# Refitting the transfer times and priorities of a planner that orders a four-layer graph network on one core

## The chip, the core and the metric

The kernel runs on one of the eight cores of a Trainium2 chip. The time is device microseconds of one launch. Five engines work side by side, each through its own instructions in order: TensorE (PE) for matrix products and transposes, VectorE (DVE), ScalarE (ACT), GpSimd (POOL), and SyncE (SP), which here only issues transfers. POOL issues some transfers too.

## The reference, cut to what matters

There are 16 graphs of 1024 nodes with 256 features, and one adjacency matrix for all. Four layers follow each other, and each adds its result to its input.

```python
for W, a in (L0, L1, L2):                        # 4, 1 and 1 heads
    h = max(layernorm(x), 0)
    q = h @ W
    e = leaky_relu(q @ a_src [:, None] + q @ a_dst [None, :])
    x = x + act(softmax(where(adj > 0, e, -big)) @ q)     # elu, relu, elu
h = max(layernorm(x), 0)                         # layer 3: a transformer block
q, k, v = split(h @ w_qkv)                       # 8 heads of 32
p = softmax(where(adj > 0, q @ k.T / sqrt(32), -1e9))
y = layernorm(h + p @ v) * g1 + c1
x = x + layernorm(y + relu(y @ w1 + b1) @ w2 + b2) * g2 + c2
```

## The kernel before

All of it is in fp32. The graphs ("batches", `b` from 0 to 15) are handled one by one, in tiles of 128 nodes (`NT` = 8) and halves of 512 nodes (`hf`).

- `gat` (layers 0 to 2) normalizes and transposes the features (L502, L531, L766), projects them (L772) and exponentiates the scores of single nodes (L783). The scores of one side become a row: PE transposes them (L838), SP writes them to DRAM (`turn_rows`, L845) and reads them back onto all 128 partitions (`spread`, L854). DVE makes the masked weights `pt` from the row (`weights`, L870). In layers 1 and 2 PE multiplies them with the features as a full array (L897). In layer 0 it runs column-tiled: four products of 32 columns stand side by side (L984 for values, L994 for the softmax's sums).
- `attention` (layer 3) keeps a copy of its input in DRAM first (`end`, L1637). `project` makes queries and keys (L1134), which are split into a high part (`hi`, L1143 on ACT) and a rest (`lo`, L1146 on DVE). Both go to a DRAM buffer `hl` (L1152), and four transfers read them back as stacks `ks` or `qs` of four 32-row pieces (L1158), so that one single-pass product of 128 rows gives a head's scores. `values` makes the values (L1172). A step is one tile of keys, one half of queries and four heads: scores (L1355), exponentials (L1379, ACT), mask (L1388, DVE), and, two steps later, values (L1220, column-tiled). For the softmax's sums, the masked weights of two or four steps are added up before one column-tiled product with ones: the first two steps on DVE (L1247), the others by an accumulating transfer from POOL's queue (L1256). In the last batch each step has its own product with ones.
- `feed` normalizes (L437 to L502), transposes, applies the two feed-forward products (L1452, with L1473 on ACT and L1490 on DVE), transposes back, reads the layer's input from DRAM (`xr`, L1505, with L1511 on DVE), normalizes again, and writes the result (L1577). `xr` has two buffers, so a read waits for an earlier write of the result.

Nothing runs in the order of this text. Every call of `pe`, `act`, `dve`, `pool` or `dma` is recorded as a piece of work with a planned duration, its operands and a stream. `Record.schedule` then simulates the five queues and gives each engine a fixed order, in which the instructions are emitted. It takes the piece that can start first; among those that can start at the same time, the one with the lowest key. What it reads:

- `KNOTS` gives each kind of stream its key along its length, added to the batch number. So 1.0 means "one batch later". "gat0" to "gat2" are layers 0 to 2, "beside" is layer 0 of batch 1 (which runs in borrowed buffers at the start), "values" is the opening of layer 3 (normalization, projections, stacks), "steps" its steps, "feed" the feed-forward, "last" that of the last batch. `LEAD` lowers the key of ACT's and DVE's pieces.
- `PASS` is the time from the planned end of a piece to the start of one on another engine that waits for it.
- `SWITCH` is what a change between column-tiled and other matmuls adds to PE's planned time. `BIAS` times it is added to the key of a piece that would need the change.
- A transfer has `moved`, for which it holds a queue common to all, and `lands`, until its data is there. `SLACK` is added to that. SP's issue takes 0.57 us in the plan, POOL's 1.135. If the queue is over `BEHIND` (2.0) behind, SP's issue takes `HELD` (1.35):

```python
queue = max(at + (us if e == "pool" else 0.2), queue) + x.moved
x.pass_on = queue + x.lands + SLACK - (at + us)
```

Of the kernel before, what the change touches and what calls it, by code (L numbers as in the profile page):

```python
# [113 lines left out]


WEIGHT = {"pe": 1.0, "dve": 0.3}
PASS = {"pe": 0.122, "act": 0.556, "dve": 0.232, "pool": 0.13, "dma": 0.0}


class Work:  # L120


    def __init__(self, engine, us, emit, key, modes, moved, lands):
        self.engine, self.us, self.emit, self.key, self.modes = engine, us, emit, key, modes
        self.pass_on = PASS[engine]
        self.moved = moved
# [9 lines left out]
def priority(x):  # L136
# [3 lines left out]
    key = base + knots[k] + (knots[k + 1] - knots[k]) * (at - k)  # L140
    return round(key - (LEAD.get(x.engine, 0.0) if lead else 0.0), 6)


class Record:
# [44 lines left out]
    def schedule(self):  # L189
        for n, x in enumerate(self.work):  # L190
# [4 lines left out]
            for y in x.before:  # L195
                y.after.append(x)
        free = dict.fromkeys(PASS, 0.0)
        queue = 0.0
        future = {e: [] for e in PASS}
        now = {e: [] for e in PASS}  # L200
        mode = "full"
# [15 lines left out]
        def turn(x):  # L217

            return BIAS * SWITCH.get((mode, x.modes[0]), 0.0) if x.engine == "pe" else 0.0

# [20 lines left out]
        while True:  # L241
            choices = [(c, e) for c, e in ((choose(e), e) for e in PASS) if c]
            if not choices:
# [16 lines left out]
            if x.moved:  # L260
                if e == "dma" and queue - at > BEHIND:
                    us = max(us, HELD)
                queue = max(at + (us if e == "pool" else 0.2), queue) + x.moved
                x.pass_on = queue + x.lands + SLACK - (at + us)
            order.append(x)
# [14 lines left out]


BEHIND, HELD = 2.0, 1.35
SLACK = 0.722
KNOTS = {
    "gat0": (-10.926, -10.742, -7.218, -4.626, -2.628, -2.099, -0.444, -3.636, -2.816),
    "gat1": (0.191, 0.25, 0.454, 0.45, 0.566, 0.582, 0.633, 1.016, 0.672),
    "gat2": (1.126, -0.076, -0.221, -0.062, 0.894, -0.428, 0.959, 1.018, 1.17),
    "beside": (1.093, 3.374, 4.836, 2.176, 5.971),
    "values": (1.444, -1.53, -3.682, -3.253, 0.902, 0.891, 2.874, 0.851, 0.421),
    "steps": (0.98, 1.188, 1.323, 1.512, 1.578, 1.712, 2.006, 2.02, 1.489),  # L290
    "feed": (2.026, 2.163, 1.768, 1.658, 2.343, 1.828, 2.009, 2.223, 3.042),
    "last": (3.521, -0.495, 0.103, 1.329, 1.339, 5.969, 5.585, 3.41, 5.439),
}
BIAS = 2.241
LEAD = {"act": 8.212, "dve": 0.635}

SWITCH = {
    ("full", "col4"): 0.137,
# [7 lines left out]
def act_us(n, pointers=0, sbuf=0):  # L306
    return (n / 1.2 + 41 + 50 * sbuf + 101 * pointers) / 1000


def tt_us(n):  # L310
    return (n / 0.96 + 67) / 1000
# [10 lines left out]
def mm_us(n):  # L322
    return 2 * max(2 * n / 2.4 + 3.0, 109) / 1000
# [5 lines left out]
def direct(ctx, tc, flag, x, adj, gat_w, gat_a, w_qkv, ln1_g, ln1_b, ln2_g, ln2_b, w1, b1, w2, b2, out):  # L329


    nc = tc.nc
# [87 lines left out]
    def pe(us, emit, w, r, modes=("full", "full")):  # L420
        rec.add("pe", us, emit, w, r, modes)

    def act(us, emit, w, r):
        rec.add("act", us, emit, w, r)

    def dve(us, emit, w, r):
        rec.add("dve", us, emit, w, r)
# [4 lines left out]
    def dma(moved, lands, emit, w, r, key=None, us=0.57, engine="dma"):  # L432
        rec.add(engine, us, emit, w, r, key=key, moved=moved, lands=lands)
# [293 lines left out]
    def gat(xt, b_mv, b_rstd, l, my):  # L727
# [120 lines left out]
        def spread(hf, h, rd):  # L848

            row = my.row.new()  # L850
            dma(
                1.2,
                2.07,
                lambda: nc.sync.dma_start(  # L854
                    row.t,
                    rd.t[h * TH : (h + 1) * TH, :]
                    .rearrange("t n -> (t n)")
                    .partition_broadcast(P),
                ),
                [row],  # L860
                [rd],
            )
            return row
# [21 lines left out]
        for hf in range(2):  # L885
            s = slice(hf * TH, (hf + 1) * TH)
            if H == 1:
                row = spread(hf, 0, rds[hf])
                pts = [weights(hf, 0, jt, row) for jt in range(NT)]
                for k in range(TH):  # L890
# [56 lines left out]
                    if l == 1:  # L947
                        last, op = ex, ALU.add
                    else:
                        dve(tt_us(C), lambda: nc.vector.tensor_add(xs, xs, ex), [xt(it)], [b_ex(0)])  # L950
                        last, op = eo, ALU.subtract
# [132 lines left out]
    def attention(b, xt, b_mv, b_rstd):  # L1084
# [42 lines left out]
        def project(g, hf, keys, stack, at):  # L1127

            sc, hi, lo = r_sc.new(), r_hi.new(), r_lo.new()
            c0 = keys * C + g * P  # L1130

            def product():
                for ct in range(CT):
                    nc.tensor.matmul(  # L1134
                        sc.t,
                        wqkv_sb[:, ct, c0 : c0 + P],
                        hT.t[:, ct, hf * HALF : (hf + 1) * HALF],
                        start=ct == 0,
                        stop=ct == CT - 1,
                    )  # L1140

            pe(CT * mm_us(HALF), product, [sc], [b_qkv] + [hT((ct, hf)) for ct in range(CT)])
            act(act_us(HALF), lambda: nc.scalar.copy(hi.t.bitcast(F32R), sc.t), [hi], [sc])  # L1143
            dve(
                tt_us(HALF),
                lambda: nc.vector.tensor_sub(lo.t, sc.t, hi.t),  # L1146
                [lo],
                [sc, hi],
            )
            hl = r_hl.new()  # L1150
            for k, part in enumerate((hi, lo)):
                dma(0.65, 1.5, lambda: nc.sync.dma_start(hl.t[:, k, :], part.t), [hl(k)], [part])  # L1152
            for a in range(4):
                k = ((0, 0, 1, 1), (0, 1, 0, 1))[keys][a]
                dma(
                    1.0,
                    1.83,
                    lambda: nc.sync.dma_start(  # L1158
                        stack.t[a * D3 : (a + 1) * D3, :, at : at + HALF],
                        hl.t[:, k, :].rearrange("(r d) n -> d r n", r=HG),  # L1160
                    ),
                    [stack((r, hf if keys else 0, a)) for r in range(HG)],
                    [hl(k)],
                )
# [28 lines left out]
        def queries(g, hf):  # L1193
            qs[g, hf] = r_qs.new()
            project(g, hf, 0, qs[g, hf], 0)
# [19 lines left out]
        steps = [(g, hf, jt) for g in range(CT) for hf in range(2) for jt in range(NT)]  # L1215
# [12 lines left out]
        def run_of(g, hf):  # L1228

            return 1 if b == NB - 1 else 4 if hf == 1 else 2  # L1230
# [4 lines left out]
        for n in range(len(steps) + LAG):  # L1235
            m = n - LAG
            if m >= 0:
                g, hf, jt = steps[m]
                if jt == 0:
                    accs[g, hf] = [r_bank.new(), r_bank.new()]  # L1240
                run = run_of(g, hf)
                if jt % run == 1:
                    sums[g, hf] = [r_sums.new() for _ in range(2)]
                    for ss, p0, p1 in zip(sums[g, hf], pas[m - 1], pas[m]):
                        dve(
                            tt_us(2 * HALF),
                            lambda: nc.vector.tensor_add(ss.t, p0.t, p1.t),  # L1247
                            [ss],
                            [p0, p1],
                        )  # L1250
                elif jt % run:
                    for ss, pt in zip(sums[g, hf], pas[m]):
                        dma(
                            2.8,
                            0.85,
                            lambda: nc.gpsimd.dma_start(ss.t, pt.t, accum_op=ALU.add),  # L1256
                            [ss],
                            [pt],
                            us=1.135,
                            engine="pool",  # L1260
                        )
                pe(
                    0.8585,
                    lambda: quad(
                        accs[g, hf][0],
                        lambda r: pas[m][r // 2].t[:, r % 2, :],
                        lambda r: va.t[:, jt, (g * HG + r) * D3 : (g * HG + r + 1) * D3],
                        jt == 0,
                        jt == NT - 1,
                    ),  # L1270
                    [accs[g, hf][0]],
                    pas[m] + [va(jt)],
                    ("col4", "col4"),
                )
                if jt % run == run - 1:
                    ss = pas[m] if run == 1 else sums[g, hf]
                    pe(
                        0.8585,
                        lambda: quad(
                            accs[g, hf][1],  # L1280
                            lambda r: ss[r // 2].t[:, r % 2, :],
                            lambda r: ones,
                            jt == run - 1,
                            jt == NT - 1,
                        ),
                        [accs[g, hf][1]],
                        ss,
                        ("col4", "col4"),
                    )
# [111 lines left out]
    def feed(b, x3, hn):  # L1401
# [95 lines left out]
        def back(hf):  # L1497
            yT = yTs[hf]
            for it in (hf * TH, hf * TH + 2):
                g, z, mvz, rstdz = r_bank.new(), r_fz.new(), r_mvz.new(), r_rstdz.new()  # L1500
                xr = r_xr.new()
                dma(
                    1.0,
                    1.83,
                    lambda: nc.sync.dma_start(xr.t, x3.t[:, it : it + 2, :]),  # L1505
                    [xr(0), xr(1)],
                    [x3(hf)],
# [763 lines left out]
```

## Time and profile before

| what | value |
|---|---|
| median of 3 runs | 4077.22 us (4068.27 to 4077.92) |
| the profiled execution | 4072.03 us, its span 4070.3 us |
| granted TensorE clock | 0.995 |
| transfers | 456.54 MB, mean 112 GB/s |
| first / last matmul | starts at 11.3 us / ends at 4059.8 us |

The span runs from the first to the last instruction of the profiled execution. "Busy" is the time in which at least one instruction of an engine runs; a transfer's issue isn't counted. Lines named L... are lines of the kernel before; the change adds and removes no line, so they are the same after it. In a list of waits, "A <- B" says that A's engine sat idle until B was done. In a timeline, the columns are start, duration, engine, line, operation and operands, and brackets hold the idle time before it and what ended it.

### The profile page before, as it was taken

What the parts mean: (1) busy time and instruction counts of PE and PEld (TensorE: products, weight loads), DVE (VectorE), ACT (ScalarE), POOL (GpSimd) and SP (SyncE); (2) the same over time, 40 slices, a digit from 0 to 9 for tenths busy, and PEclk for the clock granted to TensorE, in tenths of its full rate; (3) what the DMA queues carried; (4) which work ended last, traced back from release to release, by engine and by line L of the source; (5) the groups of instructions that cost most, each with busy time, mean ns of one, the idle gap of its engine ahead of it and who ended that gap; (6) DMA issues with size and microseconds to landing.
All of it is one profiled execution on the core that took longest, in us unless ns stands there. A gap on an engine that the chain in (4) does not pass through costs nothing.

```text
span 4070.3 us, 66071 instructions
## 1 busy us (share of the span) xinstructions
PE 4012.3 (99%) x23874; PEld 2352.0 (58%) x23874; DVE 3501.7 (86%) x5994; ACT 2666.6 (66%) x6673; POOL 621.0 (15%) x631
## 2 busy tenths in 40 slices
PE   7999999999999999999999999999999999999998
PEld 4566466564655646566564665646556465665643
DVE  7778898989989899898988989899898998989866
ACT  5467575775757767576675766757577675766765
POOL 1101111111111112111111111111111121111200
PEclk9999999999999999999999999999999999999999
DMA  3034454444545345463444544445543454624451
GB/s 128 27 103 115 126 126 109 113 104 115 124 125 123 83 117 126 115 150 76 126 110 123 127 110 113 104 115 122 127 121 82 117 128 115 150 69 121 112 137 51
DMA packets 227520, 456.54 MB, mean 112 GB/s; under 512 B 24688, under 2 KB 59760, under 8 KB 227184
## 3 DMA queue, kind: packets, MB, share of 16 engines
q1 hardware_dynamic: 192624, 326.39, 28.3%
q0 software_dynamic: 34560, 125.84, 16.2%
q8 instruction: 190, 3.11, 0.3%
q14 instruction: 146, 1.20, 0.1%
HBM read 225.25 MB, written 101.06 MB: 80 GB/s over the span
## 4 chain that ended last, share of the span: by engine, by line
PE 94%; DMA 3%; ACT 1%; DVE 1%; issue 0%; SPq 0%; DVEq 0%; ACTq 0%; POOLq 0%
PE bank L897 21%; PE bank L1220 16%; PE sc L1355 12%; PE bank L984 11%; PE bank L772 9%; PE bank L531 6%; PE sc L1134 5%; PE bank L1452 5%; PE bank L994 5%; PE sc L1172 3%; DMA sums<-pa 2%; PE sc L531 1%; DVE pt L870 1%; ACT waste L448 0%; ACT pa L1379 0%
## 5 line engine op out<-in xcount | busy, mean ns | idle before, releaser
L1388 DVE TENSOR_TENSOR pa<-pa,mask 128x1024 f32<-128x1024 f32 x1024 | 1222.7, 1219 | 166.1 <-ACT pa L1379 162.6
L1379 ACT ACTIVATE pa<-sc 128x512 f32<-128x512 f32 x2048 | 1101.6, 611 | 370.1 <-DVE sums L1247 174.4
L870 DVE SCALAR_TENSOR_TENSOR pt<-row,e,mask 128x512 f32<-128x512 f32 x1472 | 1011.9, 744 | 46.6 <-DMA row<-rd 27.7
L897 PE MATMUL bank<-qb,pt 128*128 128x257 f32 x4096 | 941.0, 380 | 0.0
L897 PEld LDWEIGHTS bank<-qb,pt 128*128 128x128 f32 x4096 | 770.6, 190 | 143.6 <-issue 20.1
L1355 PE MATMUL sc<-qs,ks 128*128 128x512 f32 x2048 | 727.9, 457 | 2.6 <-DMA hl<-hi 1.1
L1220 PE MATMUL bank<-pa,va 128*32 128x512 f32 x4096 | 515.0, 597 | 0.0
L1355 PEld LDWEIGHTS sc<-qs,ks 128*128 128x128 f32 x2048 | 361.3, 189 | 237.9 <-ACT pa L1379 82.5
L984 PE MATMUL bank<-pt,qb 128*32 128x512 f32 x3840 | 461.7, 596 | 6.5 <-DVE pt L870 6.5
L1247 DVE TENSOR_TENSOR sums<-pa,pa 128x1024 f32<-128x1024 f32 x360 | 434.1, 1220 | 16.7 <-PE bank L1220 14.2
L772 PE MATMUL bank<-w_aug,hT 128*128 128x259 f32 (+1 forms) x1504 | 373.3, 389 | 0.0
L1256 POOL DMA_DIRECT2D sums<-pa x240 | 211.5, 883 | 954.1 <-DVE pa L1388 426.6
L772 PEld LDWEIGHTS bank<-w_aug,hT 128*128 128x128 f32 x1504 | 280.3, 190 | 99.6 <-ACT qb L794 35.4
L925 ACT ACTIVATE ex<-bank,rec 128x256 f32<-128x256 f32 x256 | 121.4, 475 | 288.9 <-DVE rec L917 288.7
L984 PEld LDWEIGHTS bank<-pt,qb 128*32 128x32 f32 x3840 | 116.5, 110 | 294.8 <-issue 219.5
L1220 PEld LDWEIGHTS bank<-pa,va 128*32 128x32 f32 x4096 | 115.0, 109 | 250.6 <-issue 225.7
L994 PE MATMUL bank<-pt,e 128*32 128x512 f32 x1920 | 252.0, 593 | 0.1
L1134 PE MATMUL sc<-hTa,wqkv_sb 128*128 128x512 f32 x512 | 240.0, 596 | 0.0
L468 POOL TENSOR_TENSOR rstd<-rstd,neg_half 128x4 f32<-128x4 f32 x96 | 169.2, 1762 | 362.1 <-DVE rstd L460 362.0
L1143 ACT CAST hi<-sc 128x512 fp32r<-128x512 f32 x128 | 75.1, 587 | 211.8 <-PE sc L1134 122.0
L502 ACT ACTIVATE hn<-xh,mv,rstd 128x256 f32<-128x256 f32 x376 | 202.8, 613 | 7.5 <-DVE mv L492 4.1
L1220 PE MATMUL bank<-sums,ones 128*32 128x512 f32 x1440 | 200.5, 600 | 3.9 <-DMA sums<-pa 3.7
(152 smaller groups left out, 4501.0 us busy)
## 6 DMA issues: line engine op xcount, KB each, us to landing
sums<-pa POOLq DMA_DIRECT2D x240, 512.0 KB, 6.0
ks<-hl SPq DMA_DIRECT2D x256, 256.0 KB
qs<-hl SPq DMA_DIRECT2D x256, 256.0 KB
row<-rd SPq DMA_DIRECT2D x184, 256.0 KB
hl<-hi SPq DMA_DIRECT2D x128, 256.0 KB
hl<-lo SPq DMA_DIRECT2D x128, 256.0 KB
xh<-in_x_dram SPq DMA_DIRECT2D x32, 512.0 KB
x<-xh SPq DMA_DIRECT2D x32, 512.0 KB
```

The source lines that it names most:

```text
L531: nc.tensor.transpose(dst(k), src(k), ident[:shape, :shape])
L772: nc.tensor.matmul(g.t[:, : C + 3 * H], hT.t[:, ct, k * P : (k + 1) * P], w_aug[l][:, ct, :], start=ct == 0, stop=ct == CT - 1,)
L870: lambda: nc.vector.scalar_tensor_tensor(pt.t, row.t, e3[:, 2, jt // TH, h, jt % TH : jt % TH + 1], mask[:, jt, hf * HALF : (hf + 1) * HAL ...
L897: nc.tensor.matmul(g.t[:, : D + 1], pts[jt].t[:, k * P : (k + 1) * P], qb[:, jt, 0, :], start=jt == 0, stop=jt == NT - 1,)
L984: nc.tensor.matmul(g.t[u * D + d : u * D + d + D3, :], qb[:, j, h + u, d : d + D3], pts[u][j - jt].t, start=j == 0, stop=j == NT - 1,)
L994: nc.tensor.matmul(gd.t[c : c + D3, :], one(jt + k, h + u).to_broadcast([P, D3]), pts[u][k].t, start=jt == 0, stop=jt == NT - 2,)
L1134: nc.tensor.matmul(sc.t, wqkv_sb[:, ct, c0 : c0 + P], hT.t[:, ct, hf * HALF : (hf + 1) * HALF], start=ct == 0, stop=ct == CT - 1,)
L1220: nc.tensor.matmul(ac.t[r * D3 : (r + 1) * D3, :], columns(r), of_head(r), start=first, stop=last,)
L1247: lambda: nc.vector.tensor_add(ss.t, p0.t, p1.t),
L1355: nc.tensor.matmul(scs[r - r0].t, ks.t[:, r, jt * P : (jt + 1) * P].bitcast(F32R), q.t[:, r, :].bitcast(F32R), start=True, stop=True,)
L1379: lambda: nc.scalar.activation(pt.t[:, v, :], sc.t, AF.Exp, scale=1.0 / math.sqrt(D3)),
L1388: lambda: nc.vector.tensor_mul(pt.t, pt.t, mask[:, jt : jt + 1, i0 : i0 + HALF].to_broadcast([P, 2, HALF]),),
```

## The change

Only numbers that the planner reads are changed. Which instructions are emitted, and what each does, stays the same. Five kinds of transfer get other `moved` and `lands`: the row of scores, the write of a high or low part, the four reads of a stack, the accumulating transfer, and the read of a layer's input. All eight curves of keys change, and so do `PASS`, `SLACK`, `BIAS` and `LEAD`.

```diff
-PASS = {"pe": 0.122, "act": 0.556, "dve": 0.232, "pool": 0.13, "dma": 0.0}
+PASS = {"pe": 0.067, "act": 0.488, "dve": 0.242, "pool": 0.13, "dma": 0.0}
...
-SLACK = 0.722
+SLACK = 0.692
 KNOTS = {
-    "gat0": (-10.926, -10.742, -7.218, -4.626, -2.628, -2.099, -0.444, -3.636, -2.816),
-    "gat1": (0.191, 0.25, 0.454, 0.45, 0.566, 0.582, 0.633, 1.016, 0.672),
-    "gat2": (1.126, -0.076, -0.221, -0.062, 0.894, -0.428, 0.959, 1.018, 1.17),
-    "beside": (1.093, 3.374, 4.836, 2.176, 5.971),
-    "values": (1.444, -1.53, -3.682, -3.253, 0.902, 0.891, 2.874, 0.851, 0.421),
-    "steps": (0.98, 1.188, 1.323, 1.512, 1.578, 1.712, 2.006, 2.02, 1.489),
-    "feed": (2.026, 2.163, 1.768, 1.658, 2.343, 1.828, 2.009, 2.223, 3.042),
-    "last": (3.521, -0.495, 0.103, 1.329, 1.339, 5.969, 5.585, 3.41, 5.439),
+    "gat0": (-7.312, -4.53, -3.41, -4.841, -1.822, -0.301, 0.129, -1.248, -5.175),
+    "gat1": (-0.059, 0.15, 0.563, 0.572, 0.637, 0.706, 0.828, 0.909, 0.804),
+    "gat2": (0.909, 0.795, 0.647, 0.447, 0.883, 0.816, 0.664, 0.955, 1.033),
+    "beside": (-0.048, 0.945, 2.708, 2.827, 3.928),
+    "values": (0.436, -0.157, -3.896, -2.01, 0.718, 1.463, 1.194, -0.148, -1.52),
+    "steps": (0.888, 1.134, 1.481, 1.462, 1.63, 1.792, 2.109, 1.797, 1.607),
+    "feed": (2.034, 1.861, 1.224, 2.222, 2.01, 2.099, 2.853, 2.305, 2.94),
+    "last": (2.431, 3.84, 3.952, 4.83, 2.296, 3.947, 5.098, 5.097, 8.086),
 }
-BIAS = 2.241
-LEAD = {"act": 8.212, "dve": 0.635}
+BIAS = 1.297
+LEAD = {"act": 9.115, "dve": 1.117}
...
             dma(                        # spread: row<-rd
-                1.2,
-                2.07,
+                1.45,
+                1.75,
...
-                dma(0.65, 1.5, lambda: nc.sync.dma_start(hl.t[:, k, :], part.t), [hl(k)], [part])
+                dma(0.82, 1.67, lambda: nc.sync.dma_start(hl.t[:, k, :], part.t), [hl(k)], [part])
...
                 dma(                    # project: ks<-hl, qs<-hl
-                    1.0,
-                    1.83,
+                    1.15,
+                    2.18,
...
                         dma(            # sums<-pa
-                            2.8,
-                            0.85,
+                            2.4,
+                            2.0,
...
                 dma(                    # back: xr<-x
-                    1.0,
-                    1.83,
+                    1.3,
+                    1.6,
```

## The prediction

> **What bounds the kernel now.** I read the page's first two parts first, for the engine that is full, then the chain that ended last, then who TensorE (PE) waited for, then the timeline where those waits lie. From the page:
>
> ```profile
> span 4070.3 us, 66071 instructions
> PE 4012.3 (99%) x23874; PEld 2352.0 (58%) x23874; DVE 3501.7 (86%) x5994; ACT 2666.6 (66%) x6673; POOL 621.0 (15%) x631
> PE   7999999999999999999999999999999999999998
> PE 94%; DMA 3%; ACT 1%; DVE 1%; issue 0%; SPq 0%; DVEq 0%; ACTq 0%; POOLq 0%
> ```
>
> PE is busy from the second slice to the last but one, and 94% of the chain is PE. Since the ends of matmuls are modelled, 99% alone doesn't say that it runs at its peak. So I added up its work from the distances between starts of equal matmuls: 4096 of L897 at 0.2165 us are 887; 1492 column-tiled groups (8 matmuls of L1220, L984 or L994) at 0.860 are 1283; 2048 of L1355 at 0.231 are 473; 1536 of L772 at 0.218 to 0.222 are 337; 1024 of L1134 and L1452 at 0.429 are 439; 512 of L1172 at 0.216 are 111; 2720 transposes (L531, L838) at 0.109 are 296. Sum 3826 us, and no instruction is added or removed, so this part can't change. The other 244 us can: 58 in which PE is idle (4070.3 - 4012.3), and 186 inside "busy".
>
> Who PE waited for (us in total, times, longest):
>
> ```profile
> PE bank L531 <- DVE pa L628: 11.3, 1, 11.3
> PE bank L984 <- DVE pt L870: 6.5, 1, 6.5
> PE bank L531 <- DVE yT L1490: 6.0, 2, 3.0
> PE bank L531 <- ACT xh L502: 4.9, 1, 4.9
> ...
> PE bank L1220 <- DMA sums<-pa: 3.7, 7, 1.5
> PE bank L1452 <- ACT fz L1473: 2.6, 3, 1.4
> PE sc L1172 <- DVE lo L1146: 2.6, 2, 2.4
> PE sc L1355 <- DMA hl<-hi: 1.1, 1, 1.1
> ```
>
> Nearly all of it is at the two ends: 22.9 us before 50 us, 16.6 after 3850, and 10.5 after the last matmul. All waits on a transfer together are 5.4 us (3.7, 1.1, and 0.6 on qs). The middle, 100 to 3850 us, has no hole worth naming.
>
> The 186 us inside "busy" is mostly changes between column-tiled and other matmuls. The timeline of PE late in the last attention, where each step is two tiled groups and four scores:
>
> ```profile
> 3995.35 1.07 PE L1220 MATMUL bank<-pa,va 128*32 128x512 f32 x8
> 3996.24 1.04 PE L1220 MATMUL bank<-pa,ones 128*32 128x512 f32 x8
> 3997.21 1.19 PE L1355 MATMUL sc<-qs,ks 128*128 128x512 f32 x4
> 3998.33 1.06 PE L1220 MATMUL bank<-pa,va 128*32 128x512 f32 x8
> ```
>
> A period is 2.98 us (3998.33 - 3995.35); two groups and four scores alone are 2 x 0.860 + 4 x 0.231 = 2.64. Going into and out of the tiling thus costs 0.34 us a pair. Counted along the trace's matmuls there are 413 such pairs: 140 us, 3.4% of the span.
>
> **What the Trainium skill says.** "TensorEngine Tiling (Array Packing)", Key Properties, states that a change of tiling mode drains the array. The rows above agree, and set the price that I use: 0.34 us a pair. "Perfetto Trace Analysis", Tensor Engine Instruction, says that ACT and DVE take their instructions strictly in order, so what stands behind a waiting one waits too. The timeline of all engines shows just that in the hole at 3900 us:
>
> ```profile
> 3906.30 0.69 DVE L1511 TENSOR_TENSOR xr<-xr,row_c 128x512 f32<-128x512 f32 x1 [4.79 <-DMA xr<-x]
> 3906.91 0.16 DVE L492 SCALAR_TENSOR_TENSOR mv<-mv,rstd 128x4 f32<-128x4 f32 x1
> 3907.11 2.08 ACT L502 ACTIVATE xh<-xh,mv,rstd 128x256 f32<-128x256 f32 x4 [3.66 <-DVE mv L492]
> 3907.76 2.80 PE L531 MATMUL bank<-ident,xh 128*128 128x128 f32 x8 [4.93 <-ACT xh L502]
> ```
>
> VectorE (DVE) waits 4.79 us for a row of x; L492, whose input POOL wrote by 3902.6, stands behind it, then ACT, then PE. An order that puts L1511 there only fits a plan in which the row lands earlier; on the chip it shared the transfer engines with four stack transfers issued at 3901.89.
>
> **The change part by part.** The instructions and all emitted operands stay; only numbers that the planner reads differ. The order on every engine and queue (PE, ACT, DVE, POOL, and SP's transfers) comes out anew, and each instruction costs what its row shows, so the work sums to 0. What moves is holes and tiling pairs.
>
> *Transfer lengths and landings.* A lone transfer is planned to land 0.2 + moved + lands + SLACK after its issue. From the trace's landings: the accumulating transfer into sums lands 6.0 us (median) after issue; planned from its issue 1.135 + 2.8 + 0.85 + 0.722 = 5.5 before, 1.135 + 2.4 + 2.0 + 0.692 = 6.2 now. Four stack transfers in a row: a median 5.3 (ks) and 5.1 (qs), a tenth of ks over 8.3; the planned queue time goes from 4.0 to 4.6 a stack, the landing behind it from 1.83 to 2.18, and as an issue on SP is planned at 1.35 instead of 0.57 us once the queue is 2.0 behind, SP too is planned slower. Row: 3.27 measured; 4.2 before, 4.1 now. The new numbers are nearer to the trace. Worth: at most the 5.4 us of waits on transfers directly, and what stands behind late transfers on DVE: the 4.93 us above, and near the end 4.42 us before L1511 with L1490 behind it, which is 6.0 us of PE waits (2.9 and 3.0). If cover is gone where a later planned landing pushes stacks out, a stall like the 1.1 us one on hl comes 16 times, once a batch: -18 us on the wrong side.
>
> *Hand-overs.* PASS says what is added from one engine's end to the next's start. From starts in the trace: PE to ACT 0.20 (L772 to its reader 0.417 minus 0.217), ACT to DVE 0.15 (L1379: 0.625 minus the planned 0.477), DVE to PE 0.11 (L1388: 1.246 minus 1.134). PE-ACT-PE was planned at 0.678 and is now 0.555, true about 0.35 to 0.4; PE-DVE-PE goes from 0.354 to 0.309, true 0.31. The first keeps 0.15 us of margin, the second keeps none. The second runs some 200 times (8 L803 and 4 L1490 a batch); at 0.05 us each its loss is bounded by 10 us, and I take 0, since the PE queue has other work in the middle.
>
> *Priorities.* "values" at its first knot falls from 1.444 to 0.436, while late "steps" of the batch before stay near 2.0 to 2.1. For the last pair (batches 14 and 15) that is 15 + 1.44 against 14 + 2.0 before, 15 + 0.44 against 14 + 2.1 now: the opening of the last attention moves ahead of the rest of the batch before it, which then remains as cover in the hole at 3899 to 3911 (2.37 + 4.93 + 0.64 = 7.9 us). "last" rises from -0.5..1.3 to 3.8..4.8 in its first half: the last feed-forward goes behind all attention steps and fills the end (0.78 + 1.36 + 0.46 + 2.94 + 3.03 = 8.6 us of holes there). "beside" falls by 1 to 3, which brings the second batch's first layer earlier into the 6.5 + 1.1 us at 36 to 44 us. BIAS goes from 2.241 to 1.297: the key penalty of a tiling pair (0.137 + 0.18, times BIAS) falls from 0.71 to 0.41 of a batch, so by itself there are more pairs; lower margins and new knots act on the same choice. Bounds: 10% fewer (-14 us) to 15% more (+21). I take 0 and keep both.
>
> **Sum.** Recoverable are 7.9 + 8.6 + 7.6 + 3.7 (sums) = 27.8 us; not the 11.3 until the first mask arrives nor the 10.5 behind the last matmul. I take half, since each hole also has a chain of real latencies: -14. Span 4070.3 - 14 = 4056; the profiled execution took 4072.03, 1.7 more than its span, and the runs' median 4077.22 lies 5.2 above it. On the median: 4077.2 - 14 = 4063.
>
> **Rivals.** *No difference:* the holes at the ends are chains of latency (transfer, normalization, transposes), and a new order reshuffles them; the middle is full as before. For it: all transfer waits are 5.4 us, 0.13%. Then 4077, within 8. Against it: the DVE order in front of L492 was avoidable. *Slower by tiling pairs:* with the lower BIAS the planner changes mode more often in the middle, where PE has no hole to pay from. 50 pairs more (12%) are 17 us: 4094. It decides from 36 pairs on (12.2 / 0.34) if no hole closes, from 77 if the 14 us come. For it: the direct sign of BIAS, and every pair lies on the full engine; against it: the scheduler still charges the full 0.137 + 0.18 in its time. *It doesn't do what it says:* landings of a queue under load spread (ks: 3.9 to 8.3 between the tenths), so no constants fit; the effect is that of the first rival, 4077.
>
> **The numbers.** Forecast 0.42, no difference 0.30 (the third within it), slower 0.28. 0.3% is 12.2 us, about what a measurement of this kernel can tell from no change; the forecast's 14 lies just over it, and its own range is 4045 to 4069. The range 4036 to 4102 adds all recoverable holes with 10% fewer pairs (-42) on one side, and on the other 21 us of pairs with a few us of stalls (+25).
>
> **What would show it.** Right: PE's idle under 50 us, the waits on L502 at about 3900 and on L1490 near the end gone or halved, about 413 pairs, the wait on sums under 2 us. Wrong: pairs over 450, or holes over 1 us in the middle slices, above all on sc or sums. A gain over 30 us would mean that fewer pairs made it, which I don't count on.

## The result and the profile after

The kernel after takes 4097.47 us (median of 6 runs, 4093.95 to 4100.71). The kernel before, run beside it, takes 4073.28 us (6 runs, 4068.26 to 4077.92). The ratio is 1.0061, 95% interval 1.0049 to 1.0073: **slower by 0.6%**, where a gain of 0.3% was forecast. The profiled execution of after took 4093.95 us, its span 4091.7, which is 21.4 more than before's 4070.3. The ratios of the experiments below are each to runs of before made beside them, with medians of 4077.7 to 4079.1 us.

Engines and chain, from the page of after:

```profile
span 4091.7 us, 65792 instructions
PE 4020.6 (98%) x23874; PEld 2350.7 (57%) x23874; DVE 3497.0 (85%) x5994; ACT 2699.0 (66%) x6673; POOL 651.0 (16%) x631
PE 62%; DVE 12%; DMA 9%; ACT 6%; issue 5%; POOL 4%; SPq 0%; DVEq 0%; POOLq 0%; ACTq 0%
```

PE's share of busy time hardly moved (99% to 98%), but its share of the chain fell from 94% to 62%. That is the first sign: in after, more of the chain that ended last is work that PE waits for, on VectorE (1% to 12%), transfers (3% to 9%) and ScalarE (1% to 6%). Of the transfers' 9%, 8 are `sums<-pa`, the accumulating transfer, which had 2% in before. Who PE waited for (us in total, times, longest), in after:

```profile
PE bank L531 <- DVE pa L628: 15.0, 2, 11.3
PE bank L984 <- DVE pt L870: 8.0, 3, 7.0
PE sc L1355 <- ACT pa L1379: 7.4, 13, 1.5
PE bank L531 <- DVE yT L1490: 5.6, 16, 3.0
PE bank L897 <- DVE pt L870: 5.5, 13, 0.4
PE bank L1220 <- DMA sums<-pa: 4.2, 7, 1.0
```

What to see is the middle column. The wait of scores for ACT comes 13 times (once in before) and that of L897 on `pt` 13 times (not in before's list): these are waits of each batch, no longer of the two ends. The wait on sums comes 7 times, as in before. The wait of 4.9 us on `xh` L502 is gone. The hole at 3899 to 3911 us is indeed closed; busy time in that stretch, first before, then after (columns: length, then PE, PEld, DVE, ACT and POOL busy, PE's clock, share of transfers, GB/s):

```profile
3890.00:3920.00 30.00, 22.00 (x76) 12.49 (x78) 11.40 (x28) 12.65 (x26) 3.02 (x4) 0.77 0.67 174
3890.00:3920.00 30.00, 30.00 (x147) 18.27 (x146) 15.47 (x31) 23.05 (x57) 4.73 (x6) 1.00 0.66 159
```

PE is busy for all of the 30 us, where it was busy for 22.

To see where the time went I cut both spans at the first score product (L1355) of a batch. The starts are read from the traces.

| stretch | before, us | after, us | difference |
|---|---|---|---|
| start to first scores of batch 1 | 478.3 | 490.2 | +11.9 |
| 13 periods, batch 1 to batch 14 | 13 x 247.22 | 13 x 249.43 | +28.8 |
| batch 14 to batch 15 | 219.0 | 199.6 | -19.4 |
| batch 15 to the end | 159.1 | 159.3 | +0.2 |
| span | 4070.3 | 4091.7 | +21.4 |

The two rows of the ends and the ramp together are a gain of 7.3 us. The loss is in the steady batches, 2.21 us in each. In these, PE's idle time goes from 0.25 to 1.41 us a batch; column-tiled changes fall from 24.0 to 23.0 a batch (in the whole run from 413 pairs to 393). The remaining 1.4 us a batch (2.21 - 1.16 + 0.34 for one pair fewer) lies inside what the page calls busy. The ends of matmuls are modelled: in the product with ones of batch 9, a matmul counts as running for 0.59 us, though the next pair of the group starts 0.43 us after it where nothing is late. The pair that waits there starts 1.18 us after the one before it, so 0.75 us are lost, and the trace shows 0.58 as idle. By this difference a wait under 0.16 us there doesn't show at all. That all of the 1.4 us hides like this is likely, but not shown.

**The planner's own plan as a ruler.** Its planned start of every piece can be set beside the start in the trace. This is the kernel's own arithmetic, no measurement, but it says where the chip departs from it. Before was planned to end at 4063.2 and ended at 4070.3; PE's starts stay between 4.8 us ahead of the plan and 5.6 us behind it all along. After was planned to end at 4054.7, at 246.89 us a batch; the chip falls 2.5 us further behind in each batch, and is 37 us behind at the end. Its lag grows most at two places in each batch, about 71 us and 92 us after the batch's first scores. At both, something waits for an accumulating transfer (L1256). The timeline of after around them, in batch 9 (its first scores start at 2485.8):

```profile
2549.11 0.90 POOL L1256 DMA_DIRECT2D sums<-pa  x1 [0.17 <-issue]
2549.34 2.38 SPq L1158 DMA_DIRECT2D ks<-hl  x4
...
2556.96 1.09 ACT L1379 ACTIVATE pa<-sc 128x512 f32<-128x512 f32 x2 [2.62 <-DMA sums<-pa]
2557.61 0.98 PE L1355 MATMUL sc<-qs,ks 128*128 128x512 f32 x2 [0.57 <-ACT pa L1379]
...
2570.76 0.86 POOL L1256 DMA_DIRECT2D sums<-pa  x1 [1.63 <-DVE pt L870]
2570.95 3.61 SPq L1158 DMA_DIRECT2D ks<-hl  x4
...
2578.70 0.62 PE L1220 MATMUL bank<-sums,ones 128*32 128x512 f32 x2 [0.58 <-DMA sums<-pa]
```

In both, SP starts to issue four reads of a stack, 256 KB each, 0.2 us after POOL's 512 KB transfer, and goes on for 2.4 and 3.6 us. POOL's transfer then needs 7.8 and 7.9 us to land. From the issue of the first one until it lands (2549.1 to 2557.0), the core's transfer engines are busy all along, with POOL's queue (`software_dynamic`) and SP's (`hardware_dynamic`) side by side (packets, MB, and the time that they took as a share of the 16 engines):

```profile
q0 software_dynamic: 237, 0.84, 62.2%
q1 hardware_dynamic: 494, 0.92, 41.8%
```

Until the first has landed it holds a buffer of `pa`. ACT waits 2.62 us for that buffer, and PE for ACT. For the second, PE's product with ones waits directly.

Over batches 3 to 13, the accumulating transfers of after that have little beside them land after 4.5 us, where 6.2 was planned. The fourth of a batch (issued 63.1 us after its first scores) takes 7.59 where 6.44 was planned, and the eighth (83.6 us) takes 8.52 where 7.05 was planned (medians). A straight-line fit over all 240 gives +0.36 us for each 256 KB that SP issued in the 4.5 us *after* the accumulating transfer, +0.42 for each issued in the 4.5 us before, and +1.3 where another accumulating transfer was issued in the 4.5 us before, as is the case for the fourth and the eighth. The fit leaves a third of the scatter unexplained, and the first number is 0.26 in the kernel before, so these are rough estimates. In the plan the first number is zero by its rule: its queue is first in, first out, so a later transfer never delays an earlier one.

### The profile page after: what moved, and what is told of

It is laid out like the page before. It is cut to its first block, busy times and chain, and to the rows that moved or that the text cites. A ratio compares the mean times of both kernels' runs of the same rounds, so it can differ in the third digit from the quotient of the medians.

```text
span 4091.7 us, 65792 instructions
## 1 busy us (share of the span) xinstructions
PE 4020.6 (98%) x23874; PEld 2350.7 (57%) x23874; DVE 3497.0 (85%) x5994; ACT 2699.0 (66%) x6673; POOL 651.0 (16%) x631
## 3 DMA queue, kind: packets, MB, share of 16 engines
q14 instruction: 145, 1.18, 0.1%
## 4 chain that ended last, share of the span: by engine, by line
PE 62%; DVE 12%; DMA 9%; ACT 6%; issue 5%; POOL 4%; SPq 0%; DVEq 0%; POOLq 0%; ACTq 0%
PE bank L897 16%; PE bank L984 9%; PE bank L1220 8%; DMA sums<-pa 8%; PE sc L1355 6%; PE bank L772 5%; PE bank L994 5%; PE bank L531 4%; DVE pa L1388 4%; PE bank L1452 3%; DVE pt L870 3%; ACT pa L1379 3%; PE sc L1134 3%; PE sc L1172 2%; DVE sums L1247 2%
## 5 line engine op out<-in xcount | busy, mean ns | idle before, releaser
L1379 ACT ACTIVATE pa<-sc 128x512 f32<-128x512 f32 x2048 | 1086.7, 599 | 285.6 <-PE sc L1355 144.6
L897 PE MATMUL bank<-qb,pt 128*128 128x257 f32 x4096 | 940.0, 380 | 6.0 <-DVE pt L870 5.5
L897 PEld LDWEIGHTS bank<-qb,pt 128*128 128x128 f32 x4096 | 770.7, 190 | 147.5 <-issue 16.6
L1355 PE MATMUL sc<-qs,ks 128*128 128x512 f32 x2048 | 726.4, 459 | 7.4 <-ACT pa L1379 7.4
L1220 PE MATMUL bank<-pa,va 128*32 128x512 f32 x4096 | 526.4, 597 | 3.0 <-DVE pa L1388 3.0
L1355 PEld LDWEIGHTS sc<-qs,ks 128*128 128x128 f32 x2048 | 362.8, 188 | 252.1 <-ACT pa L1379 83.9
L1256 POOL DMA_DIRECT2D sums<-pa x240 | 211.2, 882 | 976.2 <-DVE pa L1388 416.8
L1220 PEld LDWEIGHTS bank<-pa,va 128*32 128x32 f32 x4096 | 116.9, 109 | 256.4 <-issue 218.5
L502 ACT ACTIVATE hn<-xh,mv,rstd 128x256 f32<-128x256 f32 x376 | 198.0, 597 | 39.0 <-DVE mv L492 28.2
L1015 ACT COPY ot<-bank 128x512 f32<-128x512 f32 x120 | 70.3, 586 | 229.4 <-PE bank L984 211.9
L468 POOL TENSOR_TENSOR rstd<-rstd,neg_half 128x4 f32<-128x4 f32 x96 | 136.0, 1416 | 512.1 <-DVE rstd L460 512.1
L1220 PE MATMUL bank<-sums,ones 128*32 128x512 f32 x1440 | 210.0, 600 | 4.6 <-DMA sums<-pa 4.2
```

The source lines that it names most:

```text
L897: nc.tensor.matmul(g.t[:, : D + 1], pts[jt].t[:, k * P : (k + 1) * P], qb[:, jt, 0, :], start=jt == 0, stop=jt == NT - 1,)
L1220: nc.tensor.matmul(ac.t[r * D3 : (r + 1) * D3, :], columns(r), of_head(r), start=first, stop=last,)
L1355: nc.tensor.matmul(scs[r - r0].t, ks.t[:, r, jt * P : (jt + 1) * P].bitcast(F32R), q.t[:, r, :].bitcast(F32R), start=True, stop=True,)
L1379: lambda: nc.scalar.activation(pt.t[:, v, :], sc.t, AF.Exp, scale=1.0 / math.sqrt(D3)),
```

## The experiments

**Theories.** *L (landings):* the 2.2 us a batch come from accumulating transfers that share the transfer engines with stack reads issued just after them. *P (pass-on):* `PASS` and `SLACK` now leave too little margin, so that common scatter of hand-overs adds up. Line numbers are those of the kernel that is shown; in g1 to g4 L1355 is L1369, L1379 is L1393, L1220 is L1234; there L1229 issues the accumulating transfer, L1158 the wait's transfer of 4 bytes, and L1159 the stack reads.

Two kernels halve the accumulating transfers.

```diff
- lambda: nc.gpsimd.dma_start(ss.t, pt.t, accum_op=ALU.add),
+ lambda: nc.gpsimd.dma_start(ss.t[:, 0, :], pt.t[:, 0, :], accum_op=ALU.add),
```

**e1**, this in the kernel after:

> The kernel after with every queue's order unchanged, but each accumulating transfer into sums moves only the first of its two heads (256 KB instead of 512), so half of the softmax sums' later steps are left out. Theory L (the plan of after leaves PE waiting in each batch for two accumulating transfers that land 1.2 to 1.5 us after their planned time): the batch period, 249.43 us from first scores to first scores, falls to 247.0 to 247.4, the span from 4091.7 to 4058 to 4066. Theory P (the smaller hand-over margins in PASS make PE wait for ACT and DVE throughout, transfers or not): the period stays at 249.0 to 249.5, the span at 4086 to 4092.

Measured: 4063.74 us, ratio to before 0.9962 (0.9947 to 0.9977), span 4059.5, period 247.30, close to the plan's 246.89. The fourth transfer lands after 5.84 us. L's numbers are hit. P is out as the main cause of the steady loss, since the margins are as small as in after.

**e2**, the same in the kernel before:

> The same cut of the accumulating transfers in the kernel before, its orders unchanged (again part of the sums is left out). Theory L: before follows its plan already (period 247.22 on the chip, 247.15 planned), so little is won: span 4060 to 4068 instead of 4070.3. Theory P: nothing, 4068 to 4072.

Measured: 4103.88 us, ratio 1.0066 (1.0049 to 1.0082), period 249.36: both theories missed. Half the bytes, and slower. The first line of PE's waits:

```profile
PE sc L1355 <- ACT pa L1379: 30.4, 14, 3.8
```

The eighth transfer of a batch now has 1024 KB of SP's transfers before it and 1024 KB after it within 4.5 us (medians), and lands after 9.29 us (5.77 in before), though it carries half the bytes. If L holds, the faster sums have moved the order's timing so that this one falls among the reads of a stack. g3 below tests that.

**e3**, the other side of the collision: in the kernel after each stack read brings two of its four heads (the edit of `stack.t` and `hl.t` below without its condition; the stacks are set to zero at the start, and the other two heads' pieces stay so).

> The kernel after with every order unchanged, but each of the four reads of a stack brings only two of four heads (128 KB instead of 256); the other two heads keep zeros. The accumulating transfers are whole. Theory L with sharing (an accumulating transfer is slowed by stack reads that are issued after it): the late ones land at 6.3 to 6.9 us after issue instead of 7.6 and 8.5, the period falls to 247.3 to 248.2, the span to 4062 to 4076. Theory L without sharing (the accumulating transfers are slow by themselves or behind each other): they stay at 7.2 or more, the span at 4086 to 4092. Theory P: 4086 to 4092.

Measured: 4058.52 us, ratio 0.9954 (0.9938 to 0.9971), span 4054.5, period 247.24: better than L's ranges. The fourth transfer lands after 5.90, the eighth still after 7.80, later than L said. But it is issued 1.7 us earlier in the batch than in after, and lands 0.45 us after PE has begun the product with ones, the second half of which needs it, where in after it lands 1.10 us after that (medians). So what counts is when a landing meets its reader, and not how long it took. With `PASS` and `SLACK` as in after, the plan's 4054.7 is reached. So the loss needs both sides, full sums and full stack reads.

**e4** and **e5** take this apart. In e4 the eight stack reads of group 1, first half (queries and keys), are halved, in e5 all others.

```diff
- stack.t[a * D3 : (a + 1) * D3, :, at : at + HALF],
- hl.t[:, k, :].rearrange("(r d) n -> d r n", r=HG),
+ stack.t[a * D3 : (a + 1) * D3, : (2 if (g, hf) == (1, 0) else HG), at : at + HALF],
+ hl.t[: (P // 2 if (g, hf) == (1, 0) else P), k, :].rearrange("(r d) n -> d r n", d=D3),
```

> The kernel after, all orders unchanged; only the eight stack reads of queries and keys for the first half of head group 1 bring two heads of four (the others keep zeros). These are issued while the steps of group 0's second half run, where the two late accumulating transfers lie. Sharing there: the gain of halving all stack reads (period 249.43 to 247.24, span 4091.7 to 4054.5) comes back nearly whole: period 247.2 to 247.8, span 4054 to 4064. Sharing anywhere, or the general load: at most half of it, period over 248.3, span over 4073.

> The counterpart: all other stack reads bring two heads of four, the eight for the first half of group 1 are whole. Sharing at that place: little gain, period 248.8 to 249.5, span 4078 to 4092. General load: half of the gain or more, span under 4073.

Measured: e4 4083.41 us, ratio 1.0011 (1.0002 to 1.0020), period 248.55; e5 4079.63 us, ratio 1.0000 (0.9991 to 1.0009), period 248.55. "Nearly the whole gain" was a miss for e4: it has 40% of it, and its 248.55 and its span of 4081.4 lie in the range given for "sharing anywhere". e5, with a span of 4076.0, lies between its two ranges. PE's waits say why. First e4, then e5:

```profile
PE bank L1220 <- DMA sums<-pa: 5.6, 10, 1.2
```

```profile
PE sc L1355 <- ACT pa L1379: 7.8, 14, 1.1
```

e4 cures the first collision (5.90 us) and keeps the second (8.98 us, PE waits at the product with ones). In e5 the first stays (7.66 us, scores wait for ACT), while the waits on sums fall from 4.2 to 0.5 us: the eighth lands after 7.99 us, but 0.51 us after the product's start (e4: 1.42). There are two collisions, and removing either gains about 0.9 us a batch (249.43 - 248.55), together 1.8 of the 2.2 us that e3 gains.

**Parts of the change alone**, each put into the kernel before: f_pass takes only `PASS` and `SLACK`, f_dma only the five kinds of transfer, f_prio only `KNOTS`, `BIAS` and `LEAD`.

> The kernel before with only PASS and SLACK as after. The planner gives this a planned end of 4139.9 us (before: 4063.2, which the chip exceeded by 7.1; after: 4054.7, exceeded by 37.0). Theory P: the smaller margins make the plan unreachable here too, 30 us or more over it: span 4170 to 4185. Theory L: margins alone cost little against the plan: 4135 to 4155. Either way far slower than before, since the priorities were chosen for other costs.

> The kernel before with only the five changed transfer lengths and landings of after, with the larger hand-over margins kept. Planned end 4243.7 us. Late transfers (theory L): the chip exceeds it by as much as it likes where an accumulating transfer collides, 5 to 40 us, margins or not. Smaller margins as the cause (theory P): no more than the 7 us of before, since the margins are those of before: 4240 to 4252.

> The kernel before with only the new curves of keys, BIAS and LEAD. Planned end 4300.1 us, so about 4300 to 4330: curves chosen for other costs give a far worse order. Theory P: within 7 us of the plan. Theory L: over the plan where accumulating transfers land late.

| kernel | planned end, us | span, us | time, us |
|---|---|---|---|
| f_pass | 4139.9 | 4170.8 | 4167.77, ratio 1.0221 (1.0201 to 1.0242) |
| f_dma | 4243.7 | 4265.2 | 4267.37 |
| f_prio | 4300.1 | 4395.3 | 4397.06 |

f_pass fell in P's range and missed L's. But it loses 2.3 us a batch on its plan, most of it at a product with the sums (3.9 us in every second batch), so it doesn't decide. Its first line of PE's waits:

```profile
PE bank L1220 <- DMA sums<-pa: 26.2, 11, 3.7
```

f_dma and f_prio, one run each, keep before's margins and fall behind their plans too, by 21.5 and 95 us. P alone, which allows 7 us, can't make that, and f_dma is in L's range. But f_prio's first waits are others:

```profile
PE bank L1220 <- DVE pa L1388: 41.0, 26, 5.0
PE bank L531 <- DVE rec L1040: 27.4, 17, 3.6
```

Its waits on sums add up to 14.7 us, so most of its lag of 95 us stays unexplained. More telling is the first column: the parts alone are far slower in the plan already. Curves are only good with the costs that they were chosen with, so such an undoing by parts doesn't share out the 21.4 us.

**Keep all the work, move one side.** If L is right, it is enough that the reads go out after the sums have landed. The planned order is kept; behind it, a transfer of 4 bytes from the sums, ahead of the reads on SP's queue, makes SP wait.

```diff
+ def read(a, k):
+     if keys and g == 1 and "ss" in LATEST:       # sums of the last accumulating transfer issued
+         nc.sync.dma_start(mark, LATEST.pop("ss")[0:1, 0, 0:1])
+     nc.sync.dma_start(stack.t[...], hl.t[...])   # as before
```

**g1** is this in the kernel after, **g2** in the kernel before, **g3** in e2.

> The kernel after with the same planned order and all of its work; the only edit stands behind the plan: the reads of the keys' stacks of group 1 wait, by a transfer of 4 bytes from the sums ahead of them on SP's queue, until the accumulating transfer issued before them has landed (some 30 transfers of 4 bytes more in the whole run). Theory L (each batch of the kernel after loses its 2.2 us where stack reads issued just after the accumulating transfers make these land 1 to 1.5 us late): the transfers that landed 7.6 and 8.5 us after their issue land after 5 to 6.5, the period falls from 249.4 to between 247.0 and 248.0 us a batch, the span to between 4055 and 4072, about 0.5% below the kernel after, so level with the kernel before or below it. Rival S (the stacks are needed as early as they land now, or SP's queue is): what the sums gain is lost where scores wait for stacks that come 3 to 6 us later, or where hl and row issues stand behind the wait on SP; the period stays at 249 us or goes above 250, with a new wait of scores or of copies on transfers in PE's list.

> The kernel before with the same edit as in g1: its order is unchanged, and the reads of the keys' stacks of group 1 wait until the accumulating transfer issued before them has landed. In the kernel before the late sums cost nothing that lasts (its period of 247.2 us is the planned 247.15). Theory L: no gain to be had, 247.0 to 247.5 us a batch and within 0.2% of before. Rival S: slower by what the later stacks cost, the same amount as in g1, 1 us or more a batch (above 4085).

> e2 (the kernel before, each accumulating transfer moving only the first of two heads, so that half of the later sums is left out) with the wait of g1 ahead of the stack reads of group 1. e2 was 0.7% slower than before, its last accumulating transfer of group 0 landing after 9.29 us with 1 MB of stack reads around it. Theory L: that transfer lands within 7 us, the period falls from 249.4 to 247.0 to 248.2 us, 4060 to 4080. Rival (e2's loss has another source, such as an order on VectorE or GpSimd that the earlier sums turn over): it stays at 249 us and 4095 to 4110.

| kernel | time, us | ratio to before | period, us |
|---|---|---|---|
| g1 | 4080.36 | 1.0007 (0.9999 to 1.0015) | 248.72 |
| g2 | 4058.69 | 0.9949 (0.9936 to 0.9963) | 246.41 |
| g3 | 4057.80 | 0.9947 (0.9932 to 0.9962) | 246.30 |

**g1:** L is half right, and so is S. The two late transfers land after 5.72 and 5.98 us, and most of the loss in time is gone (ratio 1.0061 to 1.0007). But the period stops at 248.72, above L's 248.0. Its first line of PE's waits, and one of its places in the timeline:

```profile
PE sc L1369 <- DMA ks<-hl: 16.4, 14, 2.0
```

```profile
2575.60 1.17 PE L1369 MATMUL sc<-qs,ks 128*128 128x512 f32 x4 [1.72 <-DMA ks<-hl]
```

The second group of reads goes out at 2567.74, after the sums, and 6.1 us later PE is free for the scores that need it: too soon, so it waits 1.72 us. The reads and the sums are both urgent there, so one of them makes PE wait.

**g2** missed both expectations, on the good side: the kernel before gains 0.5%. Its timeline around the two accumulating transfers of batch 9 that have reads behind them:

```profile
2523.30 0.90 POOL L1229 DMA_DIRECT2D sums<-pa  x1 [1.61 <-ACT pa L1393]
2528.36 0.25 SPq L1158 DMA_DIRECT2D mark<-sums  x1
2528.72 0.79 SPq L1159 DMA_DIRECT2D ks<-hl  x2
...
2547.63 0.90 POOL L1229 DMA_DIRECT2D sums<-pa  x1
2552.75 0.25 SPq L1158 DMA_DIRECT2D mark<-sums  x1
2552.81 1.08 ACT L1393 ACTIVATE pa<-sc 128x512 f32<-128x512 f32 x2 [1.53 <-DMA sums<-pa]
2553.10 1.74 SPq L1159 DMA_DIRECT2D ks<-hl  x4
```

The sums land after 5.0 and 5.1 us, and the reads follow at once. Here the stacks have time. In before the first of these places looks like this (batch 9 again):

```profile
2529.71 0.82 SPq L1158 DMA_DIRECT2D ks<-hl  x2
...
2529.99 0.90 POOL L1256 DMA_DIRECT2D sums<-pa  x1 [1.65 <-ACT pa L1379]
...
2531.15 2.28 SPq L1158 DMA_DIRECT2D ks<-hl  x2
...
2537.51 0.62 PE L1220 MATMUL bank<-sums,ones 128*32 128x512 f32 x2 [0.41 <-DMA sums<-pa]
```

So the kernel before has the same collision: this transfer lands after 7.5 us, and before's periods are 246.3 to 246.5 us in five of the thirteen and 247.4 to 248.9 in the other eight. I had taken its 247.2 for the floor, because the plan says 247.15; the plan isn't a floor. In g2 twelve of the thirteen are 246.3, and PE's idle time between 500 and 3690 us falls from 3.3 to 0.03 us. From its page:

```profile
span 4058.0 us, 66145 instructions
PE 96%; ACT 1%; DVE 1%; DMA 1%; issue 0%; SPq 0%; DVEq 0%; ACTq 0%
```

g2 computes all that before computes and is faster than both kernels of this case.

**g3** settles e2: with the wait the loss of 0.7% becomes a gain of 0.5%, a little more than L said, and the eighth transfer lands after 3.26 us in place of 9.29. With the waits in place the bytes of the sums cost nothing that can be seen here: half of them (g3) and all of them (g2) differ by 0.9 us, less than either's interval.

**g4** asks whether the two waits in after share one slack: g1 with the wait only ahead of the first group of reads, `(g, hf) == (1, 0)`.

> g1 with the wait ahead of the first of its two groups of reads alone, those of the keys' stacks of group 1, first half; the reads of the second half go out as in the kernel after. In g1 both late sums were cured, but scores then waited 1.2 us a batch for the stacks of the second half, 1.4 us with what follows. Theory L: the accumulating transfer issued 63 us after a batch's first scores lands within 6 us, the one issued at 83.6 us stays at 8 to 9 us and costs its 1.3 us a batch, and no scores wait for ks; period 248.2 to 248.6 us, span 4070 to 4082, 0.3 to 0.6% below after. Rival (the two waits are one and the same slack, so that what is not lost at the first is lost at the second): the second stall grows to 2 us or more and the period stays at 249.2 to 249.6, span at 4088 or more.

Measured: 4085.93 us, ratio 1.0017 (1.0010 to 1.0024), span 4083.1, period 248.78: 0.2 us a batch above L's range, 0.4 below the rival's. The fourth transfer lands after 5.69, the eighth after 7.92 us, no scores wait for `ks`, and the waits on sums are back:

```profile
PE bank L1234 <- DMA sums<-pa: 7.5, 13, 1.8
```

So curing the first place doesn't move the whole loss to the second. At the second, g1's wait only changed what PE waits for: 248.72 us a batch with it, 248.78 without.

## Why the prediction was wrong

- **Direction.** Faster by 14 us was forecast; it is slower by 24.2 on the medians (4097.47 - 4073.28). That the time lies within the range, near its upper end, is luck: that end was set by 15% more tiling pairs and a few us of stalls, and there are 5% fewer pairs.
- **Work.** "The work sums to 0" held: counted by the same durations, PE's products are 237.5 us a batch in both kernels.
- **Tiling pairs.** I took 413 unchanged; there are 393, which at 0.34 us is a gain of 7 us. The sign that I read off `BIAS` isn't that of the whole change; no run changes `BIAS` alone. The rival that is slower by tiling pairs is refuted: after is slower with fewer of them.
- **Priorities.** The opening of the last attention did move ahead, and the hole at 3899 to 3911 us did close: the stretch from batch 14 to 15 is shorter by 19.4 us. The holes near the end shrank from 8.7 to 5.4 us, the wait of 3.0 on L1490 staying, but one of 2.8 us opened at 3949 us. At 36 to 45 us nothing changed (7.7 us in both). What I left out is the other end of the same curves: from batch 0's first scores to batch 1's, after takes 234.2 us where before took 221.0: 13.2 more, and the plan itself has 14.0 more there. So the priorities and the ends gave 7.3 us net, half of the 14 that I took.
- **Transfer lengths: the step that failed.** I wrote "worth: at most the 5.4 us of waits on transfers directly", and named a stall "once a batch: -18 us on the wrong side", but the sum has no term for it. It even counts 3.7 us of waits on sums as recoverable. This term measures +28.8 us: two stalls in each batch, near 0.9 to 1.1 us each, where I had named one of 1.1. With the collisions taken out (e1, e3) the period is back at 247.3 and 247.2. The premise of my third rival, that landings spread under load, was right; its price, nothing, was wrong. I also compared unlike things: 6.0 us measured under load with 5.5 planned for a lone transfer. With the plan's own queue counted, its median was 6.2 us in before already, and is 6.4 in after, where 5.9 is measured. So the new constants are more cautious, not nearer (22% of the 240 accumulating transfers land later than planned, 30% in before), and I took that for safety. But it isn't the share of late ones that counts. Two in a batch land 1.2 and 1.5 us late, and they are the two with a buffer or a product waiting. And the middle that I called full held a loss already: g2 takes 0.8 us a batch off the kernel before (247.22 to 246.41).
- **Hand-overs.** Taken as 0. No run charges after's margins in after's order: e1 and e3 keep them and end 4.8 us after the plan and 0.2 ahead of it. f_pass leaves open what they would cost in another order.
- **What would show it wrong.** "Holes over 1 us in the middle slices, above all on sc or sums" pointed to the right two operands, but most of these waits are under 1 us, and more than half of the loss in a batch (1.4 of 2.56 us besides the fewer pairs) hides in modelled busy time. Idle time misleads in the same way between g1 and after: g1 has more of it in the middle (23.3 us against 18.4) and is faster.

The Trainium skill, "DMA: Bandwidth & Descriptors", Queues, rings and completion order, says that each transfer engine takes turns between the queues that have work for it, packet by packet. The traces agree with the consequence: the queues' packets stand side by side in the stretch shown above, and the two late transfers land after 7.6 and 8.5 us with SP's reads issued right after them, but after 5.7 and 6.0 us where g1 holds these reads back. I could have weighed this rule before: a plan with one queue in order can't hold it, whatever its constants are.

## What to carry to other kernels

A planned order is only as good as its model of what is shared: longer transfer times in it don't help where two queues slow each other in a way that it can't express. Look for pairs of transfers on different queues issued within a microsecond of each other, and ask which of the two has somebody waiting. Where the other has time, a wait ahead of it costs a line and here gave 0.5%; where both are urgent (g1), it only moves the wait.

## What was not expected of the hardware

- A transfer issued later delays an earlier one on another queue: by estimate about 0.4 us for each 256 KB in the kernel after and 0.3 in before (the fits over 240). In e2 a transfer of 256 KB took 9.29 us amid 2 MB of SP's transfers, and 3.26 us when the reads were held back (g3).
- Fewer bytes can be slower: e2 moves half of the later sums and loses 0.7%, because its timing brings two queues together.
- Short waits on a full PE show as busy time in good part: after's busy time is 8.3 us higher than before's (4020.6 - 4012.3), for the same products and fewer changes of tiling.
